# Two turns of the second layer: from TensorE into PSUM to VectorE in squares of 32

## The chip, the cores and the metric

The kernel runs on one core of a Trainium2 chip. A core has a matrix engine (TensorE), three engines for elementwise and similar work (VectorE, ScalarE, GpSimd), and queues that issue transfers (SyncE's among them). The engines run side by side. Each works through its own list of instructions in order, and they wait for each other through semaphores. TensorE writes its results to a small memory of eight banks, PSUM; the others read it and keep tiles in SBUF, a memory of 128 partitions.

The metric is the device time of one execution in microseconds. Names of engines in the profile: PE is TensorE's matmuls, PEld its weight loads, DVE is VectorE, ACT is ScalarE, POOL is GpSimd, SP is SyncE.

## The reference

2048 tokens (8 sequences of 256) of 128 numbers pass through four sublayers, each added to its input and then normed over the 128 numbers:

```python
x = _layernorm(x + _L0_attn_ref(x, ...), axis=-1)   # l2-normed q, k; one feature per sequence
x = _layernorm(x + _L0_ffn_ref(x, ...), axis=-1)    # router, 8 experts, two per token
x = _layernorm(x + _L1_attn_ref(x, ...), axis=-1)   # see below
x = _layernorm(x + _L1_ffn_ref(x, ...), axis=-1)    # see below
```

The first two make up what the kernel calls the first layer, the last two the second. In the second layer:

```python
def _L1_attn_ref(x, ...):
    ...                                  # two grouped convolutions, a norm
    for i in range(4):
        h = linear_attention(h, ...)     # 16 heads, rotary tables, a norm
    f = gelu(h @ W1 + b1) @ W2 + b2      # 128 -> 512 -> 128
    return layernorm(f + h, ln2_g, ln2_b)

def _L1_ffn_ref(x, ...):
    h = silu(x @ w1.T * w1_s) * (x @ w2.T * w2_s)       # 128 -> 512
    h = gelu(h @ h1.T * h1_s)                           # 512 -> 512
    h = gelu(h @ h2.T * h2_s)                           # 512 -> 512
    return h @ w3.T * w3_s                              # 512 -> 128
```

Everything is in 32-bit floating point.

## The kernel before

The first layer and the experts fill the span up to about 180 us and are not touched. The second layer (`second_layer`, called once for each of four blocks of 512 tokens) is what the change is in.

A block of activations lies in one of two ways. By feature: 128 partitions are the features, and the 512 columns the tokens; products with weights take and give this form. By token: 128 partitions are tokens, and the columns are four groups (`NT` = 4) of 128 features; norms need this form, since the statistics of VectorE (`moments_of`, lines 903 and 905) run along the columns. To get from one to the other the block is turned: `turn` (line 945 and after, the transposes at line 948) issues four 128x128 transposes on TensorE, each against the identity, into one PSUM bank.

Two of these turns matter here. Both start from a block by feature and are followed by a norm:

- Behind the attention's feed-forward: products of `W1` (L1217) and `W2` (L1228), then `sf` on VectorE (L1231: bias and residual), then the turn into `psf`, its statistics, the root on GpSimd (L335, L336), two steps on VectorE (`scaled_g`, L1240, and `add_xb`, L1249), and the norm of the sum with the block's input. The result is turned back on TensorE and copied to `xT` (L1256), from which the last feed-forward starts.
- The last one: the gated products (L1261, with L1264 on ScalarE and L1266 and L1268 on VectorE), two products of 512 by 512 (L1281, gelu at L1286), the last product (L1302), `sz` on VectorE (L1305: scale and residual), then the turn into `psz`, the statistics, the root, and the centring into `y` (`centre`, L926), which is stored (L1315).

The last block does the second of these in two halves (`parts` is 2 for it), the others whole.

The order of all instructions of the second layer is written out ahead of time by a planner (`Steps`). Each step is put into it with an engine, a cost in nanoseconds, what it reads and writes, and rings (PSUM banks, SBUF tiles) from which it takes buffers. The planner gives each step a rank: its cost and the costs behind it along the longest way to the end. Then it walks through time; of all steps that could start first it takes the one with the highest rank plus offset, so that an engine doesn't stand idle in the plan while a step for it is ready. The offset belongs to the block: a tuple of four numbers in `do`, which lets block 0 lead and the others follow. On the chip each engine keeps to the order found, whatever the real durations are.

In the attention (`attention`), L1105, L1126, L1132, L1141, L1143, L1158, L1193 and L1203 are its steps on VectorE; L1187 is the product that waits for L1158.

Of the kernel before, what the change touches and what calls it, by code (L numbers as in the profile page):

```python
# [18 lines left out]
P = 128  # L19
B, N, D = 8, 256, 128  # L20
T = B * N
NB = 4
TB = T // NB
NT = TB // P
# [197 lines left out]
def tile_network(ctx: ExitStack, tc: tile.TileContext, a: dict, out: bass.AP):  # L222
    nc = tc.nc
# [29 lines left out]
    def by_tile(ap, n=NT):  # L253
        return ap.rearrange("p (i d) -> p i d", i=n)
# [32 lines left out]
    for blk in range(NB):  # L287
        x = res()
        nc.sync.dma_start(
            out=x, in_=a["x"][blk * TB : (blk + 1) * TB, :].rearrange("(i p) d -> p i d", p=P)  # L290
# [20 lines left out]
    def col(name, i=0):  # L311
        at = COLS[name][0] + i
        return cols[:, at : at + 1]
# [283 lines left out]
    with tc.manual_schedule():  # L597
# [35 lines left out]
        n = E  # L633
# [227 lines left out]
    def chunked(ap):  # L861
        return ap[:, : FC * TB].rearrange("p (c t) -> p c t", c=FC)
# [19 lines left out]
    def second_layer(blk):  # L882
        def of(names):
            return [n if "." in n else f"{n}.{blk}" for n in names.split()]

        def do(engine, cost, run, reads="", writes="", lag=0, behind="", later=0, **new):
            plan.add(
                engine, cost, run, of(reads), of(writes) + of(" ".join(new)),
                {f"{n}.{blk}": ring for n, ring in new.items()}, lag, (0, -10000, -12500, -16500)[blk] - later, of(behind),
            )  # L890

        def T(name):
            return v[f"{name}.{blk}"]
# [4 lines left out]
        def moments_of(src, mv, n=NT, at=0, cost=1240, more=""):  # L898
            def run():
                m = small.tile([P, NT, 2], F32, tag="mv", name="mv")[:, :n]  # L900
                stats = small.tile([P, NT, 6], F32, tag="stats", name="stats")
                for i in range(n):
                    nc.vector.bn_stats(stats[:, i, :], by_tile(T(src))[:, at + i, :])  # L903
                for i in range(n):
                    nc.vector.bn_aggr(m[:, i, :], stats[:, i, :])  # L905
                keep_as(mv, m)

            do("DVE", cost * n // NT, run, f"{src} {more}", mv)

        def root_of(mv, r, eps, n=NT):  # L910
            do("POOL", 1350, lambda: keep_as(r, root(T(mv)[:, :, 1], n, ALU.add, eps)), mv, r)

        def shift_of(mv, r, sh):
            def run():
                shift = small.tile([P, NT], F32, tag="shift", name="shift")
                nc.gpsimd.tensor_scalar(shift, T(mv)[:, :, 0], -1.0, None, ALU.mult)
                nc.gpsimd.tensor_tensor(shift, shift, T(r), ALU.mult)  # L917
                keep_as(sh, shift)

            do("POOL", 620, run, f"{mv} {r}", sh)  # L920

        def centre(dst, src, mv, r, n=NT, at=0, cost=1120, out="", **new):

            def run():
                for i in range(n):
                    nc.vector.tensor_scalar(  # L926
                        by_tile(T(dst))[:, at + i, :], by_tile(T(src))[:, at + i, :], T(mv)[:, i, 0:1], T(r)[:, i : i + 1],
                        ALU.subtract, ALU.mult,
                    )

            do("DVE", cost * n // NT, run, f"{src} {mv} {r}" + (f" {dst}" if out else ""), out or ("" if dst in new else dst), **new)
# [12 lines left out]
        def turn(dst, src, n=NT, at=0, more="", behind=""):  # L944

            def run():
                for i in range(at, at + n):
                    nc.tensor.transpose(T(dst)[:, i * P : (i + 1) * P], T(src)[:, i * P : (i + 1) * P], ident)  # L948

            do("PE", 590 * n // NT, run, f"{src} {more}", behind=behind, **{dst: "ps"})  # L950

        def product(dst, w, src, step=0, of_=1, new=True, at=slice(0, TB)):
            def run():
                nc.tensor.matmul(T(dst)[:, at], lhsT=w(), rhs=src(), start=(step == 0), stop=(step == of_ - 1))

            return run
# [5 lines left out]
        n, per = NT // parts, BB // parts  # L962
# [18 lines left out]
        for h in range(parts):  # L981
            for i in range(h * n, (h + 1) * n):
                def combine(i=i):
# [6 lines left out]
                   behind="x_0.0" if blk or h else "", **({} if i else {"s": "tmp"}))  # L990
# [6 lines left out]
            if h == 0:  # L997
# [10 lines left out]
                do("DVE", 200, padded, xp="xp", wide="hid")  # L1008
            centre("x", "s", f"mvc{h}", f"rc{h}", n, h * n, out=f"x_{h}")
            turn(f"px{h}", "x", n, h * n, more=f"x_{h}", behind="pc_1.0" if blk == 1 else "")  # L1010
            at = slice(h * per, (h + 1) * per)
            do("ACT", 600 if parts == 1 else 380, lambda h=h, at=at: nc.scalar.copy(
# [16 lines left out]
        for h in range(parts):  # L1029
# [22 lines left out]
            by_batch(T("sc")), by_batch(T("pc")), col("conv2_b"), T("xp")[:, :, 2 : N + 2], ALU.add, ALU.add  # L1052
        ), f"pc xp {pcs}", sc="tmp")
        turn("psc", "sc")
        moments_of("psc", "mv0")
        root_of("mv0", "r0", 1e-12)
        centre("n0", "psc", "mv0", "r0", cost=1370, n0="tmp")
        turn("pn0", "n0")

        def affine(dst, p, g, b):  # L1060
# [166 lines left out]
        for c in range(FC):  # L1227
# [2 lines left out]
            ), f"f f{c}", "pf" if c else "", **({} if c else {"pf": "ps"}))  # L1230
        do("DVE", 740, lambda: nc.vector.scalar_tensor_tensor(  # L1231
            T("sf"), T("pf"), col("fb2"), T(hT), ALU.add, ALU.add), f"pf {hT}", sf="tmp")
        turn("psf", "sf")
        moments_of("psf", "mvf")
        root_of("mvf", "rf", 1e-12)

# [37 lines left out]
        src, last = "g", "pb"  # L1274
        for dst, w, scale in (("u", gh1, "h1_s"), ("w", gh2, "h2_s")):
            for c in range(FC):
                for i in range(FC):
                    new = {} if i else {f"p{dst}{c}": "ps"}
                    if dst == "w" and not i and not c:
# [5 lines left out]
                       behind="" if i else " ".join(f"{last}{n}" for n in range(FC)), **new)  # L1285
# [4 lines left out]
            src, last = dst, f"p{dst}"  # L1290

        parts = (1, 1, 1, 2)[blk]
        n = NT // parts
# [5 lines left out]
        for h in range(parts):  # L1299
            at = slice(h * n * P, (h + 1) * n * P)  # L1300
            for c in range(FC):
                do("PE", 853 // parts, lambda c=c, at=at, h=h: nc.tensor.matmul(  # L1302
                    T(f"pz{h}")[:, at], lhsT=g3[:, c, :], rhs=chunked(T("w"))[:, c, at], start=(c == 0), stop=(c == FC - 1)
                ), f"w w{c}", f"pz{h}" if c else "", behind="" if c else " ".join(f"{last}{n}" for n in range(FC)), **({} if c else {f"pz{h}": "ps"}))
            do("DVE", 740 // parts, lambda at=at, h=h: nc.vector.scalar_tensor_tensor(  # L1305
                T(f"sz{h}")[:, at], T(f"pz{h}")[:, at], col("w3_s"), T("xT")[:, at], ALU.mult, ALU.add
            ), f"pz{h} xT", **{f"sz{h}": "tmp"})
            turn(f"psz{h}", f"sz{h}", n, h * n)
            moments_of(f"psz{h}", f"mvz{h}", n, h * n)
            root_of(f"mvz{h}", f"rz{h}", 1e-5, n)  # L1310
            centre("y", f"psz{h}", f"mvz{h}", f"rz{h}", n, h * n, cost=1370)

            def store(h=h):
                at = blk * TB + h * n * P
                nc.sync.dma_start(  # L1315
                    out=out[at : at + n * P, :].rearrange("(i p) d -> p i d", p=P), in_=by_tile(T("y"))[:, h * n : (h + 1) * n, :]
                )

            do("SP", 600, store, "y", f"out{h}", lag=1800)
# [3 lines left out]
    for blk in range(NB):  # L1323
        second_layer(blk)
# [81 lines left out]
```

## Time and profile before

| what | value |
| --- | --- |
| time, median of 3 runs | 546.0 us (544.78 to 548.18) |
| the profiled execution: its time | 545.68 us |
| its span, from the first to the last instruction | 543.9 us |
| TensorE busy in the span | 503.1 us (93%) |
| VectorE busy | 281.5 us (52%), 945 instructions |
| ScalarE busy | 218.3 us (40%) |
| GpSimd busy | 209.0 us (38%) |
| transposes at L948 from SBUF tiles `t` | 144 |
| statistics at L903, four for a block's norm | 279 ns each from SBUF, 284 ns from PSUM |

The times of single instructions come from the profiled execution. Records of one engine can overlap: the next instruction may begin before the record of the last one ends, so a group of n instructions takes less than n times the duration of one. In the timeline a group of like instructions stands on one line with its start, its length as a whole and its count. The four statistics of a block at 349.06 us, for instance, take 0.87 us together.

### The profile page before, as it was taken

What the parts mean: (1) busy time and instruction counts of PE and PEld (TensorE: products, weight loads), DVE (VectorE), ACT (ScalarE), POOL (GpSimd) and SP (SyncE); (2) the same over time, 40 slices, a digit from 0 to 9 for tenths busy, and PEclk for the clock granted to TensorE, in tenths of its full rate; (3) what the DMA queues carried; (4) which work ended last, traced back from release to release, by engine and by line L of the source; (5) the groups of instructions that cost most, each with busy time, mean ns of one, the idle gap of its engine ahead of it and who ended that gap; (6) DMA issues with size and microseconds to landing.
All of it is one profiled execution on the core that took longest, in us unless ns stands there. A gap on an engine that the chain in (4) does not pass through costs nothing.

```text
span 543.9 us, 7739 instructions
## 1 busy us (share of the span) xinstructions
PE 503.1 (93%) x2607; PEld 331.7 (61%) x2607; DVE 281.5 (52%) x945; ACT 218.3 (40%) x506; POOL 209.0 (38%) x307
## 2 busy tenths in 40 slices
PE   5977779999999999999999999989999999999992
PEld 3664468888999463468787877744444444444442
DVE  2887414233444484379898997687405430021212
ACT  3861214233434134346786867544124211322210
POOL 1971556676544221236766667361301000000001
PEclk9955989999999999999999999999999999999997
DMA  8961755575552320000000000000000000000010
GB/s 238 330 211 28 233 193 186 173 232 173 195 195 93 87 80 1 1 0 2 2 1 1 1 2 2 0 1 1 0 1 0 0 19 1 0 0 0 1 39 19
DMA packets 22472, 37.32 MB, mean 69 GB/s; under 512 B 2944, under 2 KB 16000, under 8 KB 22304
## 3 DMA queue, kind: packets, MB, share of 16 engines
q1 hardware_dynamic: 18800, 31.42, 17.7%
q0 software_dynamic: 2368, 4.85, 2.7%
q10 hardware_dynamic: 1264, 0.54, 0.4%
q8 instruction: 21, 0.34, 0.3%
q14 instruction: 19, 0.16, 0.1%
HBM read 32.28 MB, written 4.52 MB: 68 GB/s over the span
## 4 chain that ended last, share of the span: by engine, by line
PE 49%; DVE 9%; POOL 4%; issue 3%; ACT 2%; DMA 1%; POOLq 0%; DVEq 0%; SPq 0%
PE ps L1281 20%; PE ps L1261 5%; PE ps L1302 3%; PE ps L1022 2%; PE ps L1042 2%; PE ps L1187 2%; DVE stats L903 2%; PE ps L1228 2%; PE ps L948 2%; PE ps L1217 2%; PE ps L1152 2%; PE ps L1077 2%; POOL root L336 1%; DVE t L1203 1%; PE ps L1100 1%
## 5 line engine op out<-in xcount | busy, mean ns | idle before, releaser
L335 POOL TENSOR_SCALAR root<-mv 128x4 f32<-128x4 f32 (+1 forms) x46 | 12.6, 275 | 208.0 <-DVE mv L905 206.2
L775 PE MATMUL ps<-xT,hid 128*128 128x256 f32 (+1 forms) x336 | 68.4, 356 | 4.4 <-issue 3.6
L775 PEld LDWEIGHTS ps<-xT,hid 128*128 128x128 f32 x336 | 56.8, 191 | 11.3 <-issue 4.3
L781 DVE SCALAR_TENSOR_TENSOR gate<-ps,hid,gl 128x256 f32<-128x256 f32 (+1 forms) x84 | 36.0, 450 | 51.7 <-ACT gl L780 32.6
L1281 PE MATMUL ps<-t,gh 128*128 128x512 f32 x128 | 58.4, 592 | 0.0
L1281 PE MATMUL ps<-hid,gh 128*128 128x512 f32 x128 | 58.2, 592 | 0.0
L336 POOL TENSOR_TENSOR root<-root,minus_half 128x4 f32<-128x4 f32 (+1 forms) x54 | 55.0, 1019 | 4.5
L780 ACT ACTIVATE gl<-ps,hid 128x256 f32<-128x256 f32 (+1 forms) x84 | 35.4, 452 | 42.4 <-PE ps L775 32.3
L755 POOL DMA_INDIRECT xg<-x,source x37 | 35.9, 971 | 31.0 <-PE ps L775 10.4
L799 POOL DMA_INDIRECT ys<-y,dest x37 | 36.4, 983 | 25.7 <-DVE y L794 13.9
L788 PE MATMUL ps<-hid,gate 128*128 128x128 f32 x296 | 38.9, 284 | 4.6 <-DVE gate L781 4.5
L1281 PEld LDWEIGHTS ps<-hid,gh 128*128 128x128 f32 x128 | 24.2, 190 | 29.7 <-issue 28.9
L1281 PEld LDWEIGHTS ps<-t,gh 128*128 128x128 f32 x128 | 24.0, 190 | 28.7 <-issue 28.7
L788 PEld LDWEIGHTS ps<-hid,gate 128*128 128x128 f32 x296 | 37.4, 198 | 6.6 <-DVE gate L781 5.5
L1266 DVE SCALAR_TENSOR_TENSOR t<-t,ps 128x512 f32<-128x512 f32 x16 | 10.9, 680 | 51.2 <-ACT t L1264 51.2
L937 ACT ACTIVATE t<-t,shift,root 128x128 f32<-128x128 f32 x64 | 26.4, 482 | 10.7 <-POOL shift L917 10.7
L1261 PE MATMUL ps<-featT,g 128*128 128x512 f32 x64 | 30.2, 592 | 0.0
L1264 ACT ACTIVATE t<-ps,half 128x512 f32<-128x512 f32 x16 | 11.0, 687 | 41.2 <-PE ps L1261 41.2
L1138 POOL TENSOR_TENSOR t<-t,t 128x512 f32<-128x512 f32 x16 | 20.4, 1273 | 17.3 <-DVE t L1126 17.3
L1286 ACT ACTIVATE t<-ps,cols 128x512 f32<-128x512 f32 x16 | 11.0, 687 | 36.3 <-PE ps L1281 36.2
L948 PEld LDWEIGHTS ps<-ident,t 128*128 128x128 f32 x144 | 17.2, 141 | 11.5 <-issue 7.5
L594 PE MATMUL ps<-tabs,ident 128*128 128x512 f32 x44 | 22.2, 663 | 0.0
(198 smaller groups left out, 927.0 us busy)
## 6 DMA issues: line engine op xcount, KB each, us to landing
hid<-in_experts_dram SPq DMA_DIRECT2D x21, 836.0 KB
got<-ys SPq DMA_DIRECT2D x6, 256.0 KB
counts<-in_counts_dram SPq DMA_DIRECT2D x1, 1032.0 KB
featT<-in_xT_dram SPq DMA_DIRECT2D x4, 256.0 KB
res<-in_x_dram SPq DMA_DIRECT2D x4, 256.0 KB
gh<-in_h1T_dram SPq DMA_DIRECT2D x1, 1024.0 KB
gh<-in_h2T_dram SPq DMA_DIRECT2D x1, 1024.0 KB
x<-res SPq DMA_DIRECT2D x4, 256.0 KB
```

Of the source, the lines that this page charges most:

```text
L336: nc.gpsimd.tensor_tensor(r, r, minus_half[:, :n], ALU.pow)
L594: return nc.tensor.matmul(p, lhsT=ident, rhs=tab("cos"), start=True, stop=True)
L755: landed[t] = nc.gpsimd.indirect_dma_start(out=xg[:, j, :], out_offset=None, in_=x1, in_offset=bass.IndirectOffsetOnAxis(ap=source[:, u : ...
L775: keep(nc.tensor.matmul(p[:, half * m : (half + 1) * m], lhsT=part(t, "w1", half * F + c * P, P), rhs=xT, start=True, stop=True,))
L780: keep(nc.scalar.activation(gl, p[:, m : 2 * m], AF.Gelu_apprx_tanh, bias=part(t, "b1", FC + c, 1)))
L781: keep(nc.vector.scalar_tensor_tensor(g[:, c, :m], p[:, :m], part(t, "b1", c, 1), gl, ALU.add, ALU.mult))
L788: keep(nc.tensor.matmul(p[:, j * D : (j + 1) * D], lhsT=g[:, c, j * P : (j + 1) * P], rhs=part(t, "w2", c * D, D), start=(c == 0), stop=(c ...
L799: put = nc.gpsimd.indirect_dma_start(out=ys, out_offset=bass.IndirectOffsetOnAxis(ap=dest[:, u : u + 1], axis=0), in_=y[:, j, :], in_offse ...
L937: nc.scalar.activation(by_tile(T(dst))[:, i, :], by_tile(T(src))[:, i, :], AF.Identity, bias=T(sh)[:, i : i + 1], scale=T(r)[:, i : i + 1],)
L948: nc.tensor.transpose(T(dst)[:, i * P : (i + 1) * P], T(src)[:, i * P : (i + 1) * P], ident)
L1261: do("PE", 853, lambda p=p, w=w, c=c: nc.tensor.matmul(T(f"{p}{c}"), lhsT=w[:, c * P : (c + 1) * P], rhs=T("xT"), start=True, stop=True), ...
L1281: do("PE", 853, lambda c=c, i=i, w=w, dst=dst, src=src: nc.tensor.matmul(T(f"p{dst}{c}"), lhsT=w[:, i, c * P : (c + 1) * P], rhs=chunk(src ...
```

## The change

Two turns are done in another way in blocks 0, 1 and 2: the one into `psf` and the last one, into `psz`. In block 3 they stay as they were. The new helper cuts a 128x128 transpose into sixteen squares of 32 by 32. One VectorE instruction transposes the squares at one place in all four token groups at once: it reads 32 partitions and four runs of 32 columns and writes them, each square transposed, to 32 other partitions. Sixteen such instructions make a turn. The result goes into an SBUF tile instead of a PSUM bank, and the statistics and the steps behind them read it from there. The planner counts 3300 ns on VectorE for it, where it counted 590 ns on TensorE.

The four offsets by block are other numbers.

```diff
@@ second_layer, do
-                {f"{n}.{blk}": ring for n, ring in new.items()}, lag, (0, -10000, -12500, -16500)[blk] - later, of(behind),
+                {f"{n}.{blk}": ring for n, ring in new.items()}, lag, (0, -10500, -13000, -14000)[blk] - later, of(behind),
@@ behind turn
+        def turn_by_squares(dst, src):
+
+            def run():
+                into, of = (T(n).rearrange("p (i c) -> p i c", i=NT) for n in (dst, src))
+                for a in range(0, P, 32):
+                    for b in range(0, P, 32):
+                        nc.vector.transpose(out=into[b : b + 32, :, a : a + 32], in_=of[a : a + 32, :, b : b + 32])
+
+            do("DVE", 3300, run, src, **{dst: "tmp"})
@@ behind the attention's feed-forward
-        turn("psf", "sf")
+        (turn_by_squares if blk in (0, 1, 2) else turn)("psf", "sf")
         moments_of("psf", "mvf")
@@ the last turn
-            turn(f"psz{h}", f"sz{h}", n, h * n)
+            if blk in (0, 1, 2):
+                turn_by_squares("psz0", "sz0")
+            else:
+                turn(f"psz{h}", f"sz{h}", n, h * n)
             moments_of(f"psz{h}", f"mvz{h}", n, h * n)
```

## What the change is predicted to do

> **What bounds the kernel now.** I read first the page (TensorE 93% busy, VectorE 52%), which is a mean over stages, and so asked next for busy time by stretches of the second layer, which fills the span from 186 us on. Columns: stretch; busy us and instruction count of TensorE, its weight loads, VectorE, ScalarE, GpSimd; granted clock.
> ```profile
> 186.00:240.00 54.00, 52.14 (x492) 27.16 (x491) 32.61 (x127) 18.17 (x37) 12.54 (x20) 1.00 0.11 30
> 240.00:345.00 105.00, 103.21 (x716) 82.87 (x715) 90.65 (x263) 76.87 (x184) 69.68 (x112) 1.00 0.01 1
> 345.00:365.00 20.00, 18.24 (x89) 11.26 (x88) 17.60 (x57) 10.93 (x24) 11.68 (x18) 1.00 0.00 1
> 365.00:390.00 25.00, 25.00 (x70) 11.77 (x69) 17.41 (x68) 8.15 (x14) 8.04 (x13) 1.00 0.00 0
> ...
> 445.00:500.00 55.00, 55.00 (x133) 24.58 (x132) 5.76 (x8) 14.10 (x21) 0.00 (x0) 1.00 0.02 5
> 500.00:530.00 30.00, 30.00 (x78) 13.64 (x77) 6.58 (x26) 4.79 (x7) 2.52 (x4) 1.00 0.06 18
> 530.00:543.90 13.90, 4.27 (x21) 3.31 (x19) 3.67 (x14) 0.71 (x2) 1.87 (x4) 0.78 0.07 19
> ```
> TensorE is the bound throughout, at full clock. It stands idle 1.79 us in 240 to 345 and 1.76 us in 345 to 365, and not at all from 365 to 530. VectorE is nearly as full up to 365 (86% and 88%), 70% busy to 390, and mostly idle behind that. The chain that ended last agrees (start, us, what) and shows the one place where VectorE leads it for long:
> ```profile
> 354.13 1.11 DVE t L1141
> 355.84 3.50 DVE t L1249 x4
> 359.82 1.13 PE ps L1187 x8
> ```
> That is TensorE's longest wait in the second layer: 1.76 us for the masked key-value product (L1158).
>
> **What leaves TensorE.** Six turns (two in each of blocks 0 to 2), four transposes each. The instruction row of L948 gives 273 ns for one, but records of TensorE overlap, so the price is the distance between starts, from the timeline of TensorE (start, us):
> ```profile
> 511.09 0.60 PE L948 MATMUL ps<-ident,t 128*128 128x128 f32 x4
> 511.53 1.02 PE L1302 MATMUL ps<-hid,g 128*128 128x512 f32 x2
> ```
> A turn holds up what follows by 0.44 us (439.83 to 440.27 and 520.12 to 520.55 say the same). Six of them: 2.6 us. Because the engine is full where they lie, all of it is on the path. By the durations it would be 6 x 4 x 0.273 = 6.6 us, which is wrong by the overlap.
>
> **What comes to VectorE.** Sixteen transposes for each turn, each over 32 partitions and 128 numbers a partition; 96 in all. No row of the trace is such an instruction. The nearest are statistics of 128x128 from SBUF (one input, no per-partition scalar, four in 0.87 us at 279 ns each: pitch 0.197) and the centring from SBUF to SBUF, with two scalars (four in 1.11 us, 341 ns each). From below: the statistics' pitch, 16 x 0.197 + 0.08 = 3.2 us a turn; the plan puts it at 3.3. From above: the centring's full duration, 16 x 0.341 = 5.5 us. Here a rule speaks against the change: the Trainium skill, "VectorE: DVE Perf Modes", section "Two Vector instructions with no wait between them", says that an instruction whose input or output starts in another group of 32 partitions than the last one's begins only when all earlier ones have finished. In this loop the output group changes with every instruction. Then the pitch is lost and the full duration counts: 16 x 0.279 = 4.5 us. Rows of before all start at partition 0, so they show the pitch and never the hold. By the pitch the six turns put 19 us on VectorE, by the rule 27. I take 4.5, the statistics' row with the hold, since the squares carry no scalars either; range 3.2 to 5.5.
>
> **Where it lands.** The psf turns follow `sf` (L1231), which runs at 347.67, 367.02 and 374.73 for what by priority are blocks 0, 1, 2. The psz turns follow L1305, at 430.59, 503.57 and 516.02. VectorE's timeline (start, us, idle before in brackets):
> ```profile
> 347.67 0.75 DVE L1231 SCALAR_TENSOR_TENSOR t<-ps,cols,featT 128x512 f32<-128x512 f32 x1 [1.89 <-PE ps L1228]
> 348.34 0.68 DVE L1203 TENSOR_TENSOR t<-ps,t 128x512 f32<-128x512 f32 x1
> ...
> 355.76 3.58 DVE L1249 SCALAR_TENSOR_TENSOR t<-t,root,t 128x128 f32<-128x128 f32 x4
> 359.26 0.41 DVE L1158 TENSOR_TENSOR kvh<-ps,tabs 128x256 f32<-128x256 f32 x1
> ...
> 367.02 0.75 DVE L1231 SCALAR_TENSOR_TENSOR t<-ps,cols,featT 128x512 f32<-128x512 f32 x1 [1.92 <-PE ps L1228]
> 370.31 0.69 DVE L1266 SCALAR_TENSOR_TENSOR t<-t,ps 128x512 f32<-128x512 f32 x1 [2.54 <-ACT t L1264]
> ```
> - psf of block 0: VectorE runs from 347.67 to 361.96 with no more than 0.1 us of gap. Queued behind are the last blocks' attention (L1203, L1132, L1126, L1105, L1141, L1143), and L1158, for which TensorE already waits.
> - psf of block 1: 4.5 us into 2.54 of idleness, so L1266, which frees PSUM banks, is up to 2.0 late. Block 2: VectorE is solid from 374.7 to 386.3 but for 0.2 us, and 1.46 idle behind that, so up to 3.0 late.
> - psz of block 0: three gaps (0.97, 0.83, 2.02) take 3.8 of 4.5; up to 0.7 late. psz of blocks 1 and 2: VectorE then has only the row ends to do, and TensorE's remaining work (L1281, L1302) waits for ScalarE. Nothing is charged; the cover is at least 7 us of idleness behind 504.32 and 4 behind 516.77. Without it a turn would cost its 4.5.
>
> What covers the first three on TensorE: the feed-forward products of other blocks, L1217 and L1228, eight of 0.86 us for a block, which need ScalarE and one VectorE step at their end. The chain has nine pairs of them (0.86 us each, 7.7 us) behind block 0's first L1261 at 368.53, the last at 398.33, so the order can pull some forward. The plan counts 3.3 us for a turn and makes room for that, since TensorE takes in the plan whatever can start first. It makes no room for 4.5 against 3.3, nor for L1249, which took 3.58 us here and 1.12 elsewhere beside additions on GpSimd. I charge 1.2 us for the first psf turn, whose stretch has no gap; the other two find more work behind them and are charged nothing.
>
> **The latency of the turned rows.** psf of block 0 had its statistics 1.7 us behind the end of `sf`; now 4.5, so block 0's L1261 (368.53) can move 2.8 us, under the 7.7 us of cover. Behind psz the rows waited 7.5 and 4.0 us for TensorE's turn; 4.5 is no worse.
>
> **Small things.** The statistics and the centring now read SBUF instead of PSUM: centring `y` goes from 1.37 to about 1.11 us, three times 0.26, hidden beside TensorE. Each turn gives back a PSUM bank and takes one of 21 SBUF tiles; the trace shows no wait by ring, so bounds are a few tenths either way, value nothing. No DMA is added, and SP and GpSimd lose no step.
>
> **The offsets.** Ranks sum the costs on the way to the end, so the two turns raise blocks 0 to 2 by 2 x (3300 - 590) = 5420 ahead of psf and by 2710 between the turns. Block 3 trailed block 0 by 16500; now by 14000 + 5420 = 19420 in the attention, 16710 between. Blocks 1 and 2 trail by 500 more than before. So the order of the attention is shaken but much alike: value nothing; the bounds are the idle time there, 3.6 us gone or 3.6 us more.
>
> **Sum.** Against the profiled execution (545.68 us; its span 543.9 and 1.8 around it): 545.68 - 2.6 + 1.2 = 544.3. It lay 0.3 under the median of 546.0, so 544.6 for the median.
>
> **Rivals.** A measurement of this kernel can tell about 1% from no change: under 540.5 is faster, over 551.5 slower.
> - A, as summed: 544.6, own range 542.5 to 546.5 (turns of 3.2 to 5.5 us in the one gapless stretch). 0.50.
> - B, slower: a square turn can't be interrupted, so a VectorE step that TensorE needs (L1158, L1266, L1268) lies behind it, between 347 and 390. Uncovered it costs 4.5 + 2.0 + 3.0 + 0.7 = 10.2, so 545.68 - 2.6 + 10.2 + 0.3 = 553.6; half covered 548.5. It decides once these waits pass 2.6 us together. For it: VectorE at 88% with a wait on it already, and 14 us more in 45. Against: the pairs of L1217 and L1228 that can move, and 150 us of work that hardly needs VectorE. 0.30, somewhat over half of it above 551.5.
> - C, the new order also loses the waits of 240 to 365: 544.6 - 1.2 - 3.6 = 539.8, half of it 541.6. For it: offsets and PSUM are freer. Against: VectorE is fuller exactly there. 0.12, half below 540.5.
> - D, the new order costs as much again: 544.6 + 3.6 = 548.2. 0.08, with 0.03 above 551.5.
>
> So faster 0.06, slower 0.20, within 1% 0.74. The range from 541.0 to 552.5 leaves out about 0.08 below (most of C) and 0.12 above (the upper end of B).
>
> **What would show it.** 24 fewer transposes at L948. 96 VectorE transposes: a group of 16 taking 4.5 us with starts a full duration apart confirms the hold; 3.2 says the pitch holds here too. TensorE without a gap from about 365 to the last L1302; a wait for L1158 of about 3 us near 360 under A, waits on L1266 or L1268 that sum to more than 2.6 under B. The stretch from the first L1217 to the end should be shorter by 1 to 2.6 us. I am wrong if the transposes take much more than 5.5 us a turn, or if the attention (240 to 345) takes another time.

## The result and the profile after

The changed kernel takes 553.2 us (median of 6 runs, 550.53 to 554.68), the kernel before 545.7 us (6 runs beside it, 544.75 to 548.18). The ratio on record, formed from all runs and not from the two medians, is 1.0119, with a 95% interval of 1.0099 to 1.0139: slower by 1.2%. The forecast was 544.6 us with a range up to 552.5.

The profiled execution of the changed kernel took 554.68 us, the longest of its six runs; its span is 552.9. Of the 9.0 us by which that span is longer, 1.8 lie ahead of everything that was changed: the first convolution of the second layer starts at 191.53 us instead of 189.68, and TensorE had a granted clock of 0.91 instead of 0.97 between 60 and 120 us, in the experts. To leave this out, I measure the second layer in each profile from the start of that convolution (L1022 before, L1032 after) to the end of the last centring (L926): 189.68 to 537.65 before, 191.53 to 546.69 after. That is 347.97 and 355.16 us, 7.2 us more.

First the same stretches as before, of the kernel after (columns: stretch; busy us and count of TensorE, weight loads, VectorE, ScalarE, GpSimd; granted clock).

```profile
186.00:240.00 54.00, 52.02 (x480) 28.00 (x482) 34.06 (x135) 18.72 (x37) 12.79 (x21) 1.00 0.13 37
240.00:345.00 105.00, 102.35 (x721) 83.28 (x713) 89.83 (x248) 74.75 (x181) 69.43 (x110) 1.00 0.00 1
345.00:365.00 20.00, 17.46 (x84) 10.79 (x83) 19.16 (x60) 11.90 (x25) 10.28 (x16) 1.00 0.00 0
365.00:390.00 25.00, 20.36 (x55) 9.64 (x56) 21.01 (x72) 7.70 (x13) 5.64 (x9) 0.89 0.00 1
...
445.00:500.00 55.00, 55.00 (x133) 24.58 (x132) 10.00 (x24) 11.88 (x18) 1.25 (x2) 1.00 0.02 5
500.00:530.00 30.00, 30.00 (x72) 13.26 (x71) 13.51 (x44) 5.88 (x9) 1.26 (x2) 1.00 0.03 10
```

TensorE, which stood still for 0.00 us between 365 and 390 in the kernel before, now stands still for 4.64 us there, and its clock falls to 0.89. The stretch ahead of it has 2.54 us of idleness instead of 1.76, the attention 2.65 instead of 1.79. The stretches are counted from the start of the span, and the second layer starts 1.85 us later here; shifted by that they hold the same sum of idle time. Behind 390 us TensorE has no gap up to 530, though half of the added VectorE work lies there.

VectorE's timeline of the kernel after (start, us, engine, line, operation; in brackets the idle time before) shows what stands in its queue:

```profile
349.06 5.05 DVE L958 STREAM_TRANSPOSE t<-t 32x128 f32<-32x128 f32 x16
354.14 0.69 DVE L1213 TENSOR_TENSOR t<-ps,t 128x512 f32<-128x512 f32 x1
...
365.88 0.39 DVE L1168 TENSOR_TENSOR kvh<-ps,tabs 128x256 f32<-128x256 f32 x1
...
380.27 5.04 DVE L958 STREAM_TRANSPOSE t<-t 32x128 f32<-32x128 f32 x16
385.34 0.69 DVE L1276 SCALAR_TENSOR_TENSOR t<-t,ps 128x512 f32<-128x512 f32 x1
```

A turn takes 5.05 us, not 4.5, and not the 3.3 of the plan. Behind the one into psf of block 0, L1213 runs at 354.14 instead of 348.34 (L1203 in the kernel before), and L1168, the masked key-value product, at 365.88 instead of 359.26; 1.85 us of each shift is the later start of the second layer. The third one, at 380.27, lies ahead of L1276, whose first input was ready from ScalarE at 378.66. TensorE's timeline shows what that does:

```profile
362.59 1.02 PE L1227 MATMUL ps<-featT,fw 128*128 128x512 f32 x2
366.42 1.13 PE L1197 MATMUL ps<-kvh,t 128*128 128x128 f32 x8 [2.80 <-POOL root L335]
367.38 1.82 PE L1227 MATMUL ps<-featT,fw 128*128 128x512 f32 x2
368.99 2.83 PE L1238 MATMUL ps<-hid,fw 128*128 128x512 f32 x4
...
376.82 7.11 PE L1271 MATMUL ps<-featT,g 128*128 128x512 f32 x16
386.18 0.63 PE L948 MATMUL ps<-ident,t 128*128 128x128 f32 x4 [2.24 <-DVE t L1276]
387.78 9.69 PE L1291 MATMUL ps<-hid,gh 128*128 128x512 f32 x18 [0.98 <-DVE hid L1278]
```

Three waits: 2.80, 2.24 and 0.98 us. The first is put down to a root on GpSimd, but L1168 ends at 366.27 and L1197 starts at 366.42, so it is L1168 that ended it. Ahead of the second, eight products of L1271 (16 records) have taken the eight PSUM banks, and the turn at 386.18, whose input was ready at 383.2, begins when L1276 ends at 386.03. That it waited for a bank is read from this order, not measured by itself.

And the matmuls behind the waits are slow. Two records of L1227 and four of L1238 take from 367.38 to 371.65, 4.27 us, where full speed gives 2.58 (six starts of 0.43 us). The 18 records of L1291 take 9.53 us up to the next start (397.31) instead of 7.73. Columns again as above, for short stretches:

```profile
362.00:366.00 4.00, 1.61 (x4) 0.38 (x2) 4.00 (x13) 0.69 (x1) 2.49 (x2) 1.00 0.00 0
367.48:370.89 3.41, 3.41 (x6) 1.35 (x5) 1.66 (x5) 0.69 (x1) 0.00 (x0) 0.50 0.00 0
387.96:391.37 3.41, 3.41 (x5) 1.33 (x6) 3.41 (x7) 0.00 (x0) 2.01 (x2) 0.50 0.00 0
```

The granted clock is 0.50 for 3.41 us behind the first wait, and for as long behind the other two. A TensorE at half clock counts as busy, so this loss is in no sum of waits.

The account of the second layer: idle time up to 390 us rises by 0.12 + 0.86 + 0.78 + 4.64 = 6.4 us; slow matmuls add 1.7 + 1.8 = 3.5; the six turns that TensorE no longer does take away 2.6. Together 7.3, beside 7.2 measured. It closes better than it can be trusted: in e7 and e9 below the same account leaves 0.8 us over.

### The profile page after: what moved, and what is told of

It is laid out like the page before. It is cut to its first block, busy times and chain, and to the rows that moved or that the text cites. A ratio compares the mean times of both kernels' runs of the same rounds, so it can differ in the third digit from the quotient of the medians.

```text
span 552.9 us, 7799 instructions
## 1 busy us (share of the span) xinstructions
PE 507.5 (92%) x2583; PEld 334.5 (61%) x2583; DVE 311.2 (56%) x1041; ACT 217.7 (39%) x506; POOL 208.3 (38%) x307
## 4 chain that ended last, share of the span: by engine, by line
PE 48%; DVE 14%; issue 2%; POOL 2%; DMA 1%; ACT 0%; POOLq 0%; DVEq 0%; SPq 0%
PE ps L1291 20%; PE ps L1271 4%; DVE t L958 3%; PE ps L1312 2%; PE ps L1032 2%; PE ps L1052 2%; PE ps L1098 2%; PE ps L1087 2%; DVE stats L903 2%; PE ps L1162 2%; PE ps L1197 2%; PE ps L948 2%; PE ps L1227 2%; PE ps L1110 1%; PE ps L1238 1%
## 5 line engine op out<-in xcount | busy, mean ns | idle before, releaser
L775 PE MATMUL ps<-xT,hid 128*128 128x256 f32 (+1 forms) x336 | 74.0, 372 | 8.1 <-ACT xT L766 3.8
L775 PEld LDWEIGHTS ps<-xT,hid 128*128 128x128 f32 x336 | 59.6, 200 | 17.7 <-ACT xT L766 4.3
L1291 PE MATMUL ps<-hid,gh 128*128 128x512 f32 x128 | 59.8, 607 | 1.0 <-DVE hid L1278 1.0
L1291 PE MATMUL ps<-t,gh 128*128 128x512 f32 x128 | 57.9, 592 | 0.0
L1291 PEld LDWEIGHTS ps<-hid,gh 128*128 128x128 f32 x128 | 24.8, 194 | 32.5 <-issue 29.8
L1291 PEld LDWEIGHTS ps<-t,gh 128*128 128x128 f32 x128 | 24.2, 190 | 29.7 <-issue 29.4
L788 PE MATMUL ps<-hid,gate 128*128 128x128 f32 x296 | 37.0, 276 | 0.0
L788 PEld LDWEIGHTS ps<-hid,gate 128*128 128x128 f32 x296 | 36.1, 192 | 1.2 <-DVE gate L781 0.2
L1276 DVE SCALAR_TENSOR_TENSOR t<-t,ps 128x512 f32<-128x512 f32 x16 | 10.9, 682 | 36.6 <-ACT t L1274 36.6
L958 DVE STREAM_TRANSPOSE t<-t 32x128 f32<-32x128 f32 x96 | 29.0, 303 | 1.4
L1271 PE MATMUL ps<-featT,g 128*128 128x512 f32 x64 | 29.8, 594 | 0.0
L1148 POOL TENSOR_TENSOR t<-t,t 128x512 f32<-128x512 f32 x16 | 21.9, 1372 | 13.9 <-DVE t L1136 12.0
L903 DVE BATCH_NORM_STATS2 stats<-t 128x6 f32<-128x128 f32 x120 | 26.1, 279 | 0.4
```

Source lines behind the costliest of these rows:

```text
L775: keep(nc.tensor.matmul(p[:, half * m : (half + 1) * m], lhsT=part(t, "w1", half * F + c * P, P), rhs=xT, start=True, stop=True,))
L788: keep(nc.tensor.matmul(p[:, j * D : (j + 1) * D], lhsT=g[:, c, j * P : (j + 1) * P], rhs=part(t, "w2", c * D, D), start=(c == 0), stop=(c ...
L958: nc.vector.transpose(out=into[b : b + 32, :, a : a + 32], in_=of[a : a + 32, :, b : b + 32])
L1271: do("PE", 853, lambda p=p, w=w, c=c: nc.tensor.matmul(T(f"{p}{c}"), lhsT=w[:, c * P : (c + 1) * P], rhs=T("xT"), start=True, stop=True), ...
L1291: do("PE", 853, lambda c=c, i=i, w=w, dst=dst, src=src: nc.tensor.matmul(T(f"p{dst}{c}"), lhsT=w[:, i, c * P : (c + 1) * P], rhs=chunk(src ...
```

## The experiments

Two theories. The stall theory: the loss comes of the psf turns on VectorE, which take 5 us because each transpose is held until the last one ends, lie ahead of steps that TensorE needs, and lower the clock by the waits they make. The order theory: the new offsets reorder some 350 us of work, and that order is worse whatever a square turn costs. Since the plan knows the turns only by the 3300 ns in its list, the real length of a turn can be changed while every engine's order stays the same. That is what tells the theories apart.

All times stand against runs of the kernel before on the same chip. Runs e13, e8, c1 and c2 were on a chip where the experts are faster (before takes 534.1 us there), so ratios and the length of the second layer are compared, not times. The ratio comes of all runs, the last column of a single profiled execution, which can lie at either end of them: e10's took 556.9 us (median 551.5), e5's 548.7 (median 550.9).

| kernel | us | ratio to before (95% interval) | second layer, us against before |
| --- | --- | --- | --- |
| after | 553.2 | 1.0119 (1.0099 to 1.0139) | +7.2 |
| e6, one start | 544.2 | 0.9970 (0.9953 to 0.9987) | -1.4 |
| e7, a quarter | 543.6 | 0.9948 (0.9933 to 0.9964) | -2.7 |
| e9, psf a quarter | 543.8 | 0.9955 (0.9935 to 0.9976) | -2.7 |
| e10, psz a quarter | 551.5 | 1.0087 (1.0071 to 1.0104) | +8.5 |
| e13, psf of block 0 a quarter | 537.1 | 1.0061 (1.0046 to 1.0077) | +2.6 |
| e11, wait filled | 552.2 | 1.0109 (1.0075 to 1.0143) | +6.8 |
| e1, old offsets | 558.7 | 1.0228 (1.0188 to 1.0268) | +13.1 |
| e2, new offsets alone | 554.6 | 1.0161 (1.0105 to 1.0216) | +7.6 |
| e8, ranks kept | 540.2 | 1.0112 (1.0093 to 1.0131) | +6.3 |
| e5, cost 5050 | 550.9 | 1.0094 (1.0060 to 1.0127) | +3.2 |
| c1, last turns of 0, 1, 2 | 533.0 | 0.9977 (0.9968 to 0.9986) | -1.2 |
| c2, last turns of 1, 2 | 533.3 | 0.9985 (0.9976 to 0.9994) | -0.9 |

**e6: the same order, all transposes starting at partition 0.**

```diff
-                        nc.vector.transpose(out=into[b : b + 32, :, a : a + 32], in_=of[a : a + 32, :, b : b + 32])
+                        nc.vector.transpose(out=into[:, :, b : b + 32], in_=of[:, :, a : a + 32])
```

> The kernel after, instruction for instruction in the same order, but each of the sixteen transposes of a turn runs over all 128 partitions (128 numbers each, as before), so that none starts in another group of 32 partitions than the last. The squares land in the wrong places, so the norm behind them is of other numbers. Hold theory (a changed start makes the next instruction wait for the last one's end): starts 0.20 to 0.22 us apart at unchanged durations of 0.30, 3.2 to 3.6 us a turn, and TensorE's waits between 360 and 390 shrink: 545 to 549. If transposes are as slow whatever their start: 5.05 us a turn and 551 to 554.

The row of L958 in its profile (count; minimum, median and maximum duration in ns; first and last start):

```profile
L958 DVE STREAM_TRANSPOSE t<-t x96: 267/270/313, 346.9 to 518.4; 128x128 f32<-128x128 f32 x96
```

Its first turn in VectorE's timeline:

```profile
346.93 3.20 DVE L958 STREAM_TRANSPOSE t<-t 128x128 f32<-128x128 f32 x16
```

Sixteen transposes take 3.20 us: starts (3.20 - 0.27) / 15 = 0.195 us apart. In the kernel after it is (5.05 - 0.303) / 15 = 0.316, a little over a full duration. A turn is 1.85 us shorter without the changes of group, as the hold says. Two things besides the start differ, though: a transpose covers 128 partitions here and 32 in after, and takes 270 instead of 303 ns, which wasn't expected. No run has transposes of 32 partitions that all start in one group, so that the start alone makes the difference is not shown. The kernel took 544.2 us, a little under the 545 to 549 expected. With turns of about the planned length the changed kernel is faster than before by 0.3%. The long wait ahead of L1197 is 1.83 us here, the other two together 0.2, and the clock between 365 and 390 us stays at 1.00.

**e7: the same order, four transposes for a turn.** The moves between groups of 32 partitions are left out.

```diff
-                    for b in range(0, P, 32):
-                        nc.vector.transpose(out=into[b : b + 32, :, a : a + 32], in_=of[a : a + 32, :, b : b + 32])
+                    for b in (a,):
+                        nc.vector.transpose(out=into[:, :, b : b + 32], in_=of[:, :, a : a + 32])
```

> The kernel after in the same order, but a turn is only four transposes over all 128 partitions (each square stays in its place: the moves across the groups of 32 are left out, so the result is of other numbers). Stall theory: 0.9 to 1.3 us a turn, no wait of TensorE beyond those of before, and the six turns it no longer does show: 542 to 545. Order theory: the order is the same as after's, so 549 or more.

A turn takes 0.89 us, and the second layer is shorter by 2.7 us, near the 2.6 that six turns of 0.44 us on TensorE make. TensorE's waits in the attention stay as in after (two of 1.18 and 1.11 us for L1162), against the expectation, and it stands idle 0.7 us longer in the second layer than before; that the layer is not 1.9 but 2.7 us shorter is not accounted for. So the order of after costs less than a microsecond against that of before when VectorE is quick enough. The order theory falls for this kernel.

**e9 and e10: which turns.** In e9 only the psf turns are cut to four transposes, in e10 only the psz turns; in e13 only psf of block 0. The order is after's each time.

```diff
-                    for b in range(0, P, 32):
-                        nc.vector.transpose(...)
+                    for b in (a,) if dst == "psf" else range(0, P, 32):
+                        nc.vector.transpose(out=into[:, :, b : b + 32], in_=of[:, :, a : a + 32]) if dst == "psf" else nc.vector.transpose(...)
```

(`dst == "psz0"` in e10, `dst == "psf" and blk == 0` in e13.)

> The order of after. The three turns into psf are cut to four transposes of 0.27 us (squares stay in place, so the result is of other numbers); the three into psz are the full sixteen of 5.05 us. If only the turns between 345 and 390 us hurt: 542 to 545, TensorE without a gap from 365 to 530. If the psz turns hurt as well (the one at 439 us lies ahead of L1276): 546 to 549.

> The order of after, the other way round: psz turns cut to four transposes, psf turns full. If only the psf turns hurt: 550 to 554, the waits of TensorE between 345 and 390 as in after. If the loss is shared: 546 to 549.

> The order of after; of the six turns only that into psf of block 0 is cut to four transposes. If each psf turn costs through its own wait: the 2.8 us wait for L1168 falls to 1 us or less with its slow matmuls behind it, 4 to 5 us back, and the waits at 384 to 388 stay: 547.5 to 550.5. If only the sum of VectorE's work counts: a third of the way back, 550 to 551.

The stretch from 365 to 390 us in e9 (columns as in the first table of stretches):

```profile
365.00:390.00 25.00, 25.00 (x68) 11.54 (x67) 21.57 (x82) 7.95 (x14) 8.40 (x13) 1.00 0.00 0
```

The same stretch in e10:

```profile
365.00:390.00 25.00, 19.45 (x53) 9.64 (x53) 19.77 (x71) 7.96 (x14) 3.88 (x9) 0.86 0.00 1
```

With full psz turns and quick psf turns TensorE has no gap, and the second layer is as short as with all of them quick. So the psz turns cost nothing, the one of block 0 ahead of L1276 at 439 us included. With full psf turns TensorE's idle time is all there: 7.18 us from 345 to 390, to the hundredth that of after. The profile is 1.3 us longer than after's, and its clock was low for 6.83 us at the first wait (366.58 to 373.40) instead of 3.41; by the ratios e10 is not slower than after (1.0087 and 1.0119). The same waits of e13, where psf of block 0 alone is quick, in TensorE's timeline:

```profile
350.25 1.13 PE L1197 MATMUL ps<-kvh,t 128*128 128x128 f32 x8 [0.99 <-POOL root L335]
...
368.32 0.63 PE L948 MATMUL ps<-ident,t 128*128 128x128 f32 x4 [2.25 <-DVE t L1276]
```

Cutting psf of block 0 alone gives back 7.2 - 2.6 = 4.6 us between the two profiles: its wait falls from 2.80 to 0.99, the 0.72 ahead of L1162 is gone, and no slow matmuls follow (1.7 us in after). The waits of 2.25 and 0.98 with 18 slow records (9.44 us to the next start) remain. So psf of block 0 cost 4.6 us, and those of blocks 1 and 2 about 2.2 + 1.0 + 1.8 = 5. These are prices of two executions; by the ratios of all runs (1.0119 and 1.0061) the first turn cost about 3.2 us.

**e11: useless matmuls in the first wait.**

```diff
             def numerators():
+                for _ in range(3 if (blk, l) == (3, 3) else 0): busy(t("po"))
                 for i in range(NT):
```

> The kernel after, with three matmuls of no use (0.86 us each, their result is overwritten) on TensorE in its 2.8 us wait for L1168. Clock theory (a wait of that length lowers the granted clock for what follows): the next six L1227 and L1238 take 2.6 us again instead of 4.3, the clock stays at 1.00 there, and the time falls by 1.5 to 2 us against after: 549 to 552. If the wait costs only itself: 552 to 554 and the six take the same 4.3 us.

TensorE's timeline of e11 (lines are later by one behind this edit; L594 is the added work):

```profile
360.88 2.74 PE L594 MATMUL ps<-tabs,ident 128*128 128x512 f32 x6
363.85 1.13 PE L1198 MATMUL ps<-kvh,t 128*128 128x128 f32 x8 [0.23 <-POOL root L335]
364.81 1.02 PE L1228 MATMUL ps<-featT,fw 128*128 128x512 f32 x2
365.67 1.88 PE L1239 MATMUL ps<-hid,fw 128*128 128x512 f32 x4
367.39 1.02 PE L1228 MATMUL ps<-featT,fw 128*128 128x512 f32 x2
...
383.52 11.02 PE L1292 MATMUL ps<-hid,gh 128*128 128x512 f32 x18 [0.97 <-DVE hid L1279]
```

The six records take 364.81 to 367.39, 2.58 us instead of 4.27, at a granted clock of 1.00. So the 1.7 us of slow matmuls came of the wait. The total hardly shows it (0.4 us in the second layer; the ratio's interval reaches from 1.0075 to 1.0143), because behind the second pair of waits, of the same 2.24 and 0.97 us, the clock stayed low for longer this time, 6.83 us, and it is 10.85 us to the next start instead of 9.53. The stretch (columns as in the first table of stretches):

```profile
382.81:389.64 6.83, 6.12 (x7) 2.53 (x8) 6.73 (x17) 0.55 (x1) 2.71 (x3) 0.50 0.00 0
```

The price of such a wait isn't fixed. The half of the expectation about the matmuls came true, that about the total stays undecided by the times.

**e1, e2 and e8: the offsets.** e1 is after with the old offsets, e2 is before with the new ones, e8 is after with block 3's offset such that the ranks in the attention stand as in before.

```diff
-(0, -10500, -13000, -14000)[blk]      # after
+(0, -10000, -12500, -16500)[blk]      # e1
+(0, -10000, -12500, -11080)[blk]      # e8
-(0, -10000, -12500, -16500)[blk]      # before
+(0, -10500, -13000, -14000)[blk]      # e2
```

> All six square turns, with the offsets of before. Stall theory (the square turns of 5.05 us on VectorE lie ahead of steps that TensorE waits for, and the clock falls behind each long wait): the turns still fall into the full stretch of VectorE at about 345 to 390 us, so 548 to 556, waits of TensorE there of some 3 us or more. Order theory (the loss is that of the new offsets): back at 543 to 546.

> The kernel before with the four offsets of after, no square turn. Stall theory: 544.5 to 547.5, as before within 0.3%. Order theory: 549 to 554.

> All six square turns as in after, with offsets such that the ranks in the attention stand to each other as in before: block 3 at -16500 + 5420 = -11080. Stall theory: the attention up to 345 us is as before (TensorE 103.2 of 105 us), the psf turns still stop TensorE behind it: 548 to 556. Order theory (after lost by a worse order of the attention): 543 to 546.

e1 is the slowest of all, slower even than the 548 to 556 expected, so the new offsets help the changed kernel. e2 went against the stall theory's expectation: without a square turn the new offsets cost 1.6%, with TensorE busy for 99.05 of 105 us in the attention (103.21 before). Order is worth as much as the whole effect studied here, but offsets and costs belong together: where the ranks are kept (e8), the attention is as good as before. The second layer starts 10.94 us earlier there, so this stretch of e8 is the one from 240 to 345 of before:

```profile
229.06:334.06 105.00, 103.22 (x716) 82.90 (x715) 90.59 (x263) 76.86 (x184) 69.72 (x112) 1.00 0.01 1
```

The psf turns still stop TensorE behind it, with waits of 1.62, 2.59 and 0.68 us, and the clock is at 0.50 for 6.83 us from the end of the second on.

e1 also shows that it isn't the length of a single wait alone that lowers the clock. Here are TensorE's timeline in its attention and the stretch behind (columns as in the first table of stretches):

```profile
261.90 1.48 PE L948 MATMUL ps<-ident,t 128*128 128x128 f32 x4 [0.24 <-ACT t L937]
263.93 1.67 PE L1197 MATMUL ps<-kvh,t 128*128 128x128 f32 x8 [0.55 <-POOL t L1155]
```

```profile
264.40:267.81 3.41, 3.41 (x10) 2.00 (x9) 2.31 (x6) 0.47 (x3) 1.69 (x4) 0.50 0.00 0
```

The two waits are of 0.24 and 0.55 us, and from 261.05 to the second of them TensorE did transposes only (L1210, L948), as it did between the 2.24 and the 0.98 us in after. Whether that is why the clock fell was not tested.

**e5: an honest cost in the plan.**

```diff
-            do("DVE", 3300, run, src, **{dst: "tmp"})
+            do("DVE", 5050, run, src, **{dst: "tmp"})
-(0, -10500, -13000, -14000)[blk]
+(0, -10500, -13000, -10500)[blk]
```

> The kernel after, but the plan counts 5050 ns for a square turn, and block 3's offset is raised by the 3500 that this adds to the ranks of the others (from -14000 to -10500). If the loss comes of the plan's wrong size: the order makes room, 544 to 548. If VectorE is too full there in any order: 550 to 556.

550.9 us, between the two expectations but in the second's range. By the ratios (1.0094 and 1.0119, with intervals that overlap) it is not clearly faster than after. In its profile (548.7 us, median 550.9) the second layer is 4.0 us shorter than in that of after (554.7, median 553.2); TensorE stands idle for 4.4 us from 345 to 390 instead of 7.2, and the clock is low once (3.41 us) and not twice. So the waits say that the plan's wrong size explains a part, and the times leave open how much. What remains is a wait of 3.3 us for L926, the centring of a block's rows ahead of their way back to TensorE, with the low clock behind it (0.93). VectorE is busy for 44 of the 45 us from 345 to 390. Only one set of offsets was run with this cost; that no order hides the psf turns is not shown.

**c1 and c2: only the last turns.** The psf turns stay on TensorE. c1 has squares in the last turn of blocks 0, 1 and 2, c2 in that of blocks 1 and 2. Offsets make up for the 2710 that such a turn adds to a block's ranks.

```diff
-        (turn_by_squares if blk in (0, 1, 2) else turn)("psf", "sf")
+        turn("psf", "sf")
-(0, -10500, -13000, -14000)[blk]      # after
+(0, -10000, -12500, -13790)[blk]      # c1
+(0, -12710, -15210, -16500)[blk]      # c2, with blk in (1, 2) at the last turn
```

> Only the last turns of blocks 0, 1 and 2 by squares, those into psf on TensorE. Offsets such that the ranks ahead of the last turn stand to each other as in before: block 3 at -16500 + 2710 = -13790, the others as before. If psz turns cost nothing where they lie: three turns of 0.44 us less on TensorE, 543.5 to 546.0, a ratio of 0.996 to 0.999. If the one of block 0 (at about 431 us, ahead of L1268) stops TensorE: 546 to 549.

> Only the last turns of blocks 1 and 2 by squares, where VectorE is idle; offsets of blocks 1 and 2 lowered by 2710, so that TensorE's order is that of before but for the two turns. Two turns of 0.44 us less: a ratio of 0.997 to 0.999, about 545.5. If rows that come 3 us later or earlier hurt: 547 or more.

Both are faster than both kernels: by 1.2 us in the second layer for three turns of 0.44 us, by 0.9 for two. In c2, from VectorE's timeline, a turn of full length in a stretch where nothing waits for it:

```profile
491.86 0.75 DVE L1315 SCALAR_TENSOR_TENSOR t<-ps,cols,featT 128x512 f32<-128x512 f32 x1 [8.04 <-PE ps L1312]
492.64 5.05 DVE L958 STREAM_TRANSPOSE t<-t 32x128 f32<-32x128 f32 x16
```

## Why the prediction was wrong

- **2.6 us off TensorE: right.** c1 and c2 show it best, with TensorE's idle time as before: 1.2 us for three turns and 0.9 for two. e7 and e9 are 2.7 us shorter, though TensorE stands idle 0.7 us longer in them.
- **4.5 us a turn (3.2 to 5.5): right in kind, 12% small.** Measured 5.05: starts 0.316 us apart, a full duration and no pitch, as the rule of the hold says (e6 agrees, with the reserve above). The duration was 303 ns and not the statistics' 279.
- **psz turns cost nothing: right,** for block 0 as well (e9, c1).
- **"I charge 1.2 us for the first psf turn ... the other two find more work behind them and are charged nothing": this step failed.** In the profiles they cost 4.6 and about 5 us (the first 3.2 by the ratios), against quick turns in the same order. The wait for L1168 itself grew by 1.04 us, from 1.76 to 2.80, close to the charge; but with a quick turn it would have been 0.99, and the matmuls behind it ran slow for another 1.7. The wait of 2.24 us behind the third turn, with the 0.98 that follows it, was charged nothing. Two things were wrong in it. First, the cover was counted in matmuls that could move, nine pairs, as if TensorE could take them while it waits. Its order is fixed in the plan, and the plan counted 3.3 us where 5.05 passed, and 1.15 for L1259, which took 3.14 beside two additions on GpSimd (1.11 without). By then the pairs had been placed elsewhere, and ahead of the second wait eight products stood in a row that needed all banks, which, as read from the order, only the delayed VectorE step could free. Second, even with the right cost in the plan (e5) the kernel is slower than before (ratio 1.0094; 3.2 us in its profile): VectorE is full from 345 to 390, and a centring that comes late is itself what TensorE waits for.
- **A term was missing: the clock.** Nothing in the sum priced what a wait does to the matmuls behind it. It is 3.5 of the 10 us lost. The Trainium skill ("TensorE: Matmul & The Clock Gate", section "Why this matters for your kernels") warns of idle gaps over about 3 us; here waits of 2.80 and of 2.24 + 0.98 us were enough, and once in e1 much shorter ones. The kernel before had only one of 1.76 and stayed at 1.00, as e6 did with 1.83. Each low stretch of 3.41 us at half clock takes about 1.7 us of work.
- **The offsets at nothing: nearly right, for the reason given.** The attention lost 0.9 us in after; by e8 against e1 the ranks were what mattered. But the bounds of 3.6 us either way were far too narrow for offsets that don't fit the costs: e2 lost 7.6.
- **Rival B named the mechanism** and its threshold, more than 2.6 us of waits together, and its uncovered price was 553.6. The sum came out near for another reason: 6.4 us more of idleness, where it had 10.2 of lateness, and 3.5 of low clock, which it had not. At a chance of 0.30 it stood behind A, because the cover was believed.

## What to carry to other kernels

Work moved to an engine that is not the bound is free only where nobody waits behind it. The same 5 us turn cost nothing on an idle VectorE and nearly 5 us on a full one, ten times the 0.44 us that it saved. Where engines keep to an order planned ahead, work that could move is no cover for a step that takes longer than the plan says; and a wait that lowers the clock costs more than its length: 1.7 us more for each 3.41 us at half clock here.

## What the runs showed of the hardware that was not expected

- A wait of TensorE of 2.80 us, and one of 2.24 us followed by one transposed block and another 0.98 us, brought the granted clock to 0.50 behind them; so did 2.59 us in e8 and 3.31 in e5, but not 1.62 (e8), 1.76 (before) or 1.83 (e6). In e1 it fell once behind waits of 0.24 and 0.55 us among transposes.
- The low clock lasted for 3.41 or 6.83 us, and for different times behind like waits: behind the 2.80 us 3.41 in after and 6.83 in e10, behind the 2.24 + 0.98 us 3.41 in after and 6.83 in e11. Nor did it set in at a fixed time: 3.87 us after the wait of 2.80 us began in after, 2.06 us after it began in e10. What decides this was not tested. So 18 records took 9.53, 10.85 or 9.44 us (after, e11, e13) instead of 7.73.
- VectorE transposes of 32 partitions that change their group of 32 start 0.316 us apart at 303 ns each; those of 128 partitions, which all start at partition 0, 0.195 apart at 270, for the same count of numbers in a partition.
